# One region of fixed instruction order over the scans and output pipelines of a two-layer state-space kernel, with the pipelines' x chunks moved to the low end of SBUF

## The chip, the cores and the metric

The kernel runs on one core of a Trainium2 chip. The metric is device microseconds for one execution. The time before is the median of three runs. Profiles come from one further execution, with times counted from the start of its span.

## The reference, cut to what matters

Eight images of 64 x 64 pixels and 96 channels pass through two layers. Each layer normalizes over groups of channels, runs a selective scan in four directions over a map of 192 channels, normalizes over the channels, gates and projects back, and adds its input:

```python
x = x + _L0_conv_ref(_gn(x), ...)
x = x + _L1_conv_ref(_gn(x), ...)

# inside a layer, for the map xc (after projection, 3x3 convolution and silu):
dA = jnp.exp(d_t[..., None] * A)
h = dA * h + d_t[..., None] * B_e * u_t[..., None]     # over 4096 positions, 4 directions
y = sum(h * C_e)
y = _layernorm(y, norm_g, norm_b)
return y * _silu(z) @ out_proj_w.T
```

Layer 1 writes its scan with a cumulative sum, and only the first positions of each direction contribute beyond the skip term. The kernel computes those positions (4 x 160 of an image) as one "short" unit; everything else of layer 1 is its convolution, the skip term and the output.

## The kernel before, in words

**Stages.** After `begin` (the convolution and the first steps of image 0) a loop runs over the images. For image `b` it calls `scan_rows`, the scan of layer 0 for image `b` with the short unit of layer 1 for image `b - 1`, and then `between`, which calls `out_phase`: the output pipeline of layer 0 for image `b` and, from `b = 1` on, of layer 1 for image `b - 1`. `finish` takes the place of `between` for the last image. There are seven calls of `between`; the first has one stream, the other six have two.

**The scan.** Work comes in sets of 128 partitions (32 channels x 4 states) by 1024 positions, 384 sets for an image and 24 short ones (640 positions). For each set ACT makes `decay` (L801), DVE makes `set` by a product (L835; GpSimd does one set in four, L825) and scans it (L846; short sets L838 and L841), GpSimd multiplies by `c_rep` (L863), and PE sums over the states into `acc` (L887), which ACT copies to the map `y` (L918, short ones L907 to `y_short`). For each group of four sets ACT first copies `dtu_rep` to `drive` (L818). SP loads `dt_rep` and `dtu_rep` five sets ahead (L481) and `b_rep` and `c_rep` four ahead (L495), 512 KB each. At the end of the short unit, SP stores `y_short` to `ys_far` (L910): this is SP's last instruction of the scan.

**The pipeline.** `out_phase` cuts a map of 4096 positions into eight chunks of 512, so it has 16 chunks with two streams. Step `k` runs each stage for chunk `k` minus its lag: sum (GpSimd L1503, lag 0), mean (PE L1439, lag 1), centre (DVE L1516), square (ACT L1482), variance (PE L1460, lag 3), x load (SP L1568, lag 5), gates (PE L1453, lag 7), scale (DVE L1520, lag 8), affine (ACT L1487, lag 9), product (GpSimd L1512, lag 9), projection (PE L1472, lag 10), the last add (DVE L1611 for layer 0, L1557 for layer 1, lag 10) and the store (lag 11; SP L1613 for layer 0, ACT's queue L1558 for layer 1). A plan puts further stages at steps: the loads of the next image's map from `xc_far` (L1689, the first at step 0), its first projection (PE L514, step 2) and deltas (L556 to L619), the loads of `ys` and of `y1` (L1673, L1627), statistics of image `b + 2` (L1716), and the stages of the next group norms (L169, L179), the last of which, "root", stands at step 23 with a table load before it.

**What sets the order.** Inside `scan_rows` and inside `out_phase` a region `tc.manual_schedule()` makes each engine and queue issue its instructions in the order in which the program emits them. Each of these calls was a region of its own. Instructions outside them (the loads of `avg`, `pick` and `zw` at the head of `out_phase`, the memsets of `edged` at L1032), and where one region's instructions fall among those of the next on an engine, were left to the scheduler.

**Where things lie.** Pools are stacked from the low end of SBUF, those with `side="right"` from the high end. In the scan the low end holds, in this order, `rows` (`x_dbl0`), `beside` (`edged`, short tiles, `conv_out`), `piece` (states, `dt0`, `z0`, `ln0`, `dtu0`) and `work` (`set`, `out`); the loads are at the high end. In `between` the low end holds `behind` (`y1`, 32 KB of a partition) and then `final` (`pick`, `avg`, `zw`, x chunks in seven buffers of 2 KB, `sz`, `r`); the pool `before`, passed to `out_phase` as `brief`, is at the high end. A tile that takes the place of another waits until the last reader of that one is done.

The few lines that set the order:

```python
for k in range(max(n + 12, max(plan, default=0) + 1)):
...
    for stage, lag in order:
        if 0 <= k - lag < n:
            stage(k - lag)
...
    for stage in plan.pop(k, []):
        stage()
```

Of the kernel before, what the change touches and what calls it, by code (L numbers as in the profile page):

```python
# [8 lines left out]
F32 = mybir.dt.float32  # L9
# [6 lines left out]
NB, HH, WW, C = 8, 64, 64, 96  # L16
L = HH * WW
NH = 2
D = NH * C
# [3 lines left out]
MM = 512  # L23
# [24 lines left out]
def two_ss2d_layers(ctx: ExitStack, tc: tile.TileContext, t: dict, out: bass.AP):  # L48
# [13 lines left out]
    nc = tc.nc  # L62

    const = ctx.enter_context(tc.tile_pool(name="const", bufs=1))
    keep = ctx.enter_context(tc.tile_pool(name="keep", bufs=2))
# [72 lines left out]
    def load_late(pool, *names):  # L138
        for name in names:
            w[name] = pool.tile(list(t[name].shape), F32, name=f"w_{name}")  # L140
            nc.sync.dma_start(w[name], t[name])  # L141
# [1230 lines left out]
    def out_phase(*streams, plan=None, brief=None):  # L1372
# [9 lines left out]
        with (  # L1382
# [7 lines left out]
            chunks = L // MM  # L1390
            n = len(streams) * chunks
            brief = brief or pool
            load_late(pool, "avg", "pick")
            zw, zb = [], []
            for l, *_ in streams:
                zw.append(pool.tile([C, D], F32, name=f"zw{l}"))
                nc.sync.dma_start(zw[-1], t[f"in{l}"][:, D:])
                zb.append(pool.tile([C, NH], F32, name=f"zb{l}"))
            plan = plan(pmm) if plan else {}
# [155 lines left out]
    def finish_second(norm, y, chunk, dst):  # L1555
        def done(i, ps, x):
            nc.vector.tensor_tensor(x, ps, x, ALU.add)  # L1557
            return lambda: nc.scalar.dma_start(dst[:, i * MM : (i + 1) * MM], x)  # L1558

        return 1, norm, y, chunk, done  # L1560
# [1 line left out]
    def kept(x1T):  # L1562
        return lambda i, pool: x1T[:, i * MM : (i + 1) * MM]

    def loaded(src):
        def chunk(i, pool):
            x = pool.tile([C, MM], F32, name="x_in", bufs=7)
            nc.sync.dma_start(x, src[:, i * MM : (i + 1) * MM])  # L1568
            return x

        return chunk
# [32 lines left out]
                norm0[1] = first_norm(1, bank)  # L1604
        return xc, parts

    def finish_first(b, y, st):


        def done(i, ps, x):  # L1610
            nc.vector.tensor_tensor(x, ps, x, ALU.add)  # L1611
            chunk_stats(st, i, x)
            return lambda: nc.sync.dma_start(x1[b][:, i * MM : (i + 1) * MM], x)  # L1613

        return 0, norm0[b], y, loaded(t["x"][b]), done

    def short_sum(b, pool, brief, put):

        y1 = pool.tile([C, NH, L], F32, name="y1")
        ys = brief.tile([C, NH, HN], F32, name="ys")  # L1620
        rows = T // WW
        full, part = divmod(HEAD, HH)
        by_col = y1.rearrange("p h (a b) -> p h b a", b=WW)

        def load(i):
            at = slice(i * T, (i + 1) * T)
            nc.sync.dma_start(y1[:, :, at], xc1_far[b][:, :, at])  # L1627

        def scale(h, i):
            at = y1[:, h, i * T : (i + 1) * T]  # L1630
            nc.scalar.mul(at, at, w["dsum1"][:, h : h + 1])

        def patch(i):
            def add(dst, src):
                nc.vector.tensor_tensor(dst, src, dst, ALU.add)

            def segment(k, start, n):
                return ys[:, :, k * HEAD + start : k * HEAD + start + n]

            def columns(k, start):  # L1640
                cols = segment(k, start, full * HH).rearrange("p h (b a) -> p h b a", a=HH)
                return cols[:, :, :, at]

            at = slice(i * rows, (i + 1) * rows)
            if i == 0:
                add(y1[:, :, :HEAD], segment(0, 0, HEAD))
            if i == NT - 1:
                add(y1[:, :, L - HEAD :], segment(2, 0, HEAD))
            add(by_col[:, :, :full, at], columns(1, 0))
            add(by_col[:, :, WW - full :, at], columns(3, part))  # L1650
            if at.stop <= part:
                add(by_col[:, :, full, at], segment(1, full * HH + at.start, rows))
            if at.start >= HH - part:
                start = at.start - (HH - part)
                add(by_col[:, :, WW - full - 1, at], segment(3, start, rows))

        put(1, nc.sync.dma_start, ys, ys_far[b])
        for i in range(NT):
            put(1 + 2 * i, load, i)
            put(6 + 2 * i, scale, 0, i)  # L1660
            put(7 + 2 * i, scale, 1, i)
            put(7 + 2 * i, patch, i)
        return y1

    def second_of(b, pool, brief, put):

        return finish_second(norm1[b], short_sum(b, pool, brief, put), loaded(x1[b]), out[b])

    def planner():
        plan = {}  # L1670
# [6 lines left out]
    def between(b, y):  # L1677

        st = stats_tile()
        xc = keep.tile([C, NH, L], F32, name="map")  # L1680
        with (
            tc.tile_pool(name="before", bufs=1, side="right") as before,
            tc.tile_pool(name="behind", bufs=1) as pool,
        ):
            plan, put = planner()

            def load(i):
                at = slice(i * T, (i + 1) * T)
                nc.sync.dma_start(xc[:, :, at], xc_far[b + 1][:, :, at])  # L1689

            put(0, load, 0)
            streams = [finish_first(b, y, st)]
            if b >= 1:
                streams.append(second_of(b - 1, pool, before, put))
            for i in range(1, NT):
                put(7 + 2 * i, load, i)
            found = {}

            def beside(pmm):
                bank = lambda name: pmm.tile([P, MM], F32, tag="mm", name=name)  # L1700
                found["parts"], stages = first_deltas(b + 1, xc, before, pmm)
                steps = (2, 3, 3, 4) + (4, 5, 5, 6, 6, 7, 7, 6, 8, 9, 9)
                steps += (8, 9, 9, 10, 10, 11, 12, 14, 15, 16, 16) + (11, 12, 12, 13)
                for step, stage in zip(steps, stages, strict=True):
                    put(step, stage)
                stages, found[1] = group_norm_stages(st, bank)
                put(23, nc.scalar.preload_act_table_set, "natural_log_exp_and_others")
                for step, stage in zip((17, 18, 19, 20, 21, 23), stages, strict=True):
                    put(step, stage)
                if b + 2 < NB:  # L1710
                    ahead = stats_tile()
                    pieces = []

                    def piece(i):
                        pieces.append(before.tile([C, MM], F32, name="x_st", bufs=3))
                        nc.sync.dma_start(pieces[i], t["x"][b + 2][:, i * MM : (i + 1) * MM])  # L1716

                    for i in range(L // MM):
                        put(i + 3, piece, i)
                        put(i + 5, lambda i: chunk_stats(ahead, i, pieces[i]), i)  # L1720
                    stages, found[0] = group_norm_stages(ahead, bank)
                    for step, stage in zip((13, 14, 15, 16, 17, 18), stages, strict=True):
                        put(step, stage)
                return plan

            out_phase(*streams, plan=beside, brief=before)
            for kind, norm, image in ((1, norm1, b), (0, norm0, b + 2)):
                if kind in found:
                    norm[image] = tuple(found[kind][x] for x in ("gm", "r", "shift"))
        return xc, found["parts"]  # L1730

    def finish(b, y):

        st = stats_tile()
        with tc.tile_pool(name="behind", bufs=1) as pool:
            plan, put = planner()
            streams = [finish_first(b, y, st)]
            if b >= 1:
                streams.append(second_of(b - 1, pool, pool, put))
            out_phase(*streams, plan=lambda pmm: plan)  # L1740
        with tc.tile_pool(name="x1T", bufs=1) as pool1:
            x1T = pool1.tile([C, L], F32, name="x1T")
            nc.sync.dma_start(x1T, x1[b])
            xc = keep.tile([C, NH, L], F32, name="map")
            norm = conv_second(x1T, st, xc)
            with rotating():
                scan_head(xc, worst)
            out_phase(finish_second(norm, xc, kept(x1T), out[b]))
# [30 lines left out]
    x1 = dram.tile([NB, C, L], F32, name="x1")  # L1779
    xc_far, xc1_far, ys_far, xs, norm0, norm1 = ({} for _ in range(6))  # L1780
    xc, parts = begin()
    for b in range(NB):
        y = keep.tile([C, NH, L], F32, name="map")
        with (
            tc.tile_pool(name="rows", bufs=1) as rows,
            tc.tile_pool(name="beside", bufs=1) as pool,
        ):
            scan_rows(xc, y, parts, beside(b, pool), rows, pool)
        if b + 1 < NB:
            xc, parts = between(b, y)  # L1790
    finish(NB - 1, y)


# [98 lines left out]
```

## Time and profile before

| | us |
|---|---|
| median of 3 runs (12752.65 to 12780.65) | 12758.46 |
| the profiled execution | 12772.51 |
| its span | 12770.7 |
| DVE busy in it | 11379.4 (89%) |
| GpSimd busy | 10766.4 (84%) |
| ACT busy | 9763.0 (76%) |
| PE busy | 9506.4 (74%) |
| DMA queue of SP, share of 16 engines | 42.9% |

The boundaries between stages are read from the timeline: the last L863 (GpSimd) of a scan ends it, and the first L846 (DVE) begins the next. For the seven calls of `between`, in order:

| boundary | last L863 ends | first L846 starts | between them |
|---|---|---|---|
| 0 (one stream) | 1470.29 | 1567.63 | 97.3 |
| 1 | 2968.91 | 3126.45 | 157.5 |
| 2 | 4535.85 | 4690.75 | 154.9 |
| 3 | 6094.15 | 6247.41 | 153.3 |
| 4 | 7654.79 | 7806.21 | 151.4 |
| 5 | 9226.95 | 9380.58 | 153.6 |
| 6 | 10794.66 | 10948.80 | 154.1 |

In timeline lines an engine's name with a q (SPq, ACTq) is its queue, which issues DMAs; such a line shows the issue and not the transfer. A number in brackets at the end is the idle time of the engine before the instruction, with what ended it.

### The profile page before, as it was taken

To read this page: it belongs to the slowest core of one execution; us is meant where nothing else is said; L and a number is where in the kernel's file an instruction comes from. 1 tells how busy PE (TensorE), PEld (TensorE's weight loads), DVE (VectorE), ACT (ScalarE), POOL (GpSimd) and SP (SyncE) were. 2 spreads that over 40 slices of the span, in tenths; PEclk is the share of its full clock that TensorE was granted. 3 is DMA by queue.
4 is the path that set the end of the run, shared out by engine and by line. 5 is a ranking of instruction groups with operands and counts; after the bars stand their busy time and mean duration, and the time that the engine had idled before them with its cause. 6 is when DMAs were issued, how large, how long until landed. Compare 5 with 4: busy or idle time off the path is not lost. (4 is left out here: it accounts for less than half of the span.)

```text
span 12770.7 us, 135094 instructions
## 1 busy us (share of the span) xinstructions
PE 9506.4 (74%) x44284; PEld 2995.9 (23%) x44284; DVE 11379.4 (89%) x7387; ACT 9763.0 (76%) x14977; POOL 10766.4 (84%) x4884
## 2 busy tenths in 40 slices
PE   5875588876888678886787758888588885886556
PEld 1221122222222222222222212222122221222112
DVE  6999799997999979999799997999889998899976
ACT  4888788786787778877788867888678886788864
POOL 3999799986999869997799977999779996899964
PEclk8877688887887778877888878878688876887766
DMA  3444444443444444443444434444344443444430
GB/s 97 161 157 157 135 164 162 160 148 109 163 159 159 147 127 164 161 159 127 132 161 159 159 121 156 154 151 158 127 145 161 160 157 113 141 162 155 156 94 24
DMA packets 653799, 1839.45 MB, mean 144 GB/s; under 512 B 174408, under 2 KB 177870, under 8 KB 652989
## 3 DMA queue, kind: packets, MB, share of 16 engines
q1 hardware_dynamic: 645917, 1818.14, 42.9%
q10 hardware_dynamic: 7168, 12.59, 0.3%
q8 instruction: 351, 5.75, 0.2%
q14 instruction: 363, 2.97, 0.1%
HBM read 1524.94 MB, written 305.52 MB: 143 GB/s over the span
## 5 line engine op out<-in xcount | busy, mean ns | idle before, releaser
L863 POOL TENSOR_TENSOR out<-set,c_rep 128x1024 f32<-128x1024 f32 x3240 | 7472.8, 2325 | 1026.5 <-DVE set L846 342.1
L846 DVE TENSOR_TENSOR_SCAN set<-decay,state,set 128x1024 f32<-128x1024 f32 x2304 | 5365.2, 2345 | 415.1 <-ACT decay L801 182.0
L801 ACT ACTIVATE decay<-dt_rep,w_a 128x1024 f32<-128x1024 f32 x3240 | 3553.4, 1097 | 571.3 <-DVE set L846 330.7
L835 DVE TENSOR_TENSOR set<-drive,b_rep 128x1024 f32<-128x1024 f32 x2430 | 2864.3, 1179 | 27.5 <-DMA out<-x_in 16.3
L887 PE MATMUL acc<-out,w_gather 128*32 128x256 f32 x25920 | 2413.1, 485 | 548.2 <-ACT y_short L907 394.5
L955 PE MATMUL ps_conv<-edged,taps 96*96 96x512 f32 (+1 forms) x4032 | 2470.6, 752 | 42.9 <-ACT z L569 39.4
L825 POOL TENSOR_TENSOR set<-dtu_rep,b_rep 128x1024 f32<-128x1024 f32 (+1 forms) x810 | 1898.1, 2343 | 58.2 <-DMA dt_far<-ln 23.4
L846 DVE TENSOR_TENSOR_SCAN set<-decay,set 128x1024 f32<-128x1024 f32 x768 | 1743.3, 2285 | 148.1 <-ACT decay L801 78.5
L878 PE MATMUL acc<-map,w_eye 96*32 96x256 f32 x4608 | 567.1, 574 | 1480.5 <-ACT map L918 1244.1
L918 ACT COPY map<-acc 32x256 f32<-32x256 f32 x3072 | 1471.2, 479 | 49.9 <-PE acc L887 9.6
L887 PEld LDWEIGHTS acc<-out,w_gather 128*32 128x32 f32 x25920 | 843.6, 133 | 2539.2 <-issue 1459.8
L955 PEld LDWEIGHTS ps_conv<-edged,taps 96*96 96x96 f32 (+1 forms) x4032 | 724.8, 199 | 1390.9 <-issue 1218.7
L857 ACT COPY state<-set 128x1 f32<-128x1 f32 x2304 | 426.4, 185 | 776.8 <-DVE set L846 770.0
L588 PE MATMUL ps_sp<-z,w_eye 96*96 96x512 f32 x960 | 652.3, 767 | 286.9 <-ACT ln L597 243.3
L609 POOL TENSOR_TENSOR dtu<-ln,map 96x1024 f32<-96x1024 f32 x256 | 670.9, 2621 | 218.7 <-DVE ln L605 132.1
L818 ACT COPY drive<-dtu_rep 128x1024 f32<-128x1024 f32 (+1 forms) x810 | 796.9, 984 | 19.2 <-DVE set L835 10.9
L556 PE MATMUL ps_dt<-x_dbl,w_dtw 7*96 7x512 f32 x1024 | 593.7, 661 | 196.8 <-ACT z L569 150.4
L878 PEld LDWEIGHTS acc<-map,w_eye 96*32 96x32 f32 x4608 | 101.3, 121 | 1936.5 <-ACT map L918 1633.0
L588 PE MATMUL ps_sp<-dtu,w_eye 96*96 96x512 f32 x960 | 555.4, 663 | 0.0
L588 PE MATMUL ps_sp<-ln,w_eye 96*96 96x512 f32 x960 | 531.3, 637 | 0.0
L588 PE MATMUL ps_sp<-dt,w_eye 96*96 96x512 f32 x960 | 502.8, 606 | 0.0
L568 ACT ACTIVATE dt<-ps_dt 96x512 f32<-96x512 f32 x512 | 303.3, 592 | 250.5 <-PE ps_dt L556 231.8
(228 smaller groups left out, 9591.5 us busy)
## 6 DMA issues: line engine op xcount, KB each, us to landing
dt_rep<-dt_far SPq DMA_DIRECT2D x768, 512.0 KB
dtu_rep<-dtu_far SPq DMA_DIRECT2D x768, 512.0 KB
b_rep<-x_dblr SPq DMA_DIRECT2D x256, 512.0 KB
c_rep<-x_dblr SPq DMA_DIRECT2D x256, 512.0 KB
b_rep<-x_dblc SPq DMA_DIRECT2D x256, 512.0 KB
c_rep<-x_dblc SPq DMA_DIRECT2D x256, 512.0 KB
dt_far<-ln SPq DMA_DIRECT2D x256, 384.0 KB
dtu_far<-dtu SPq DMA_DIRECT2D x256, 384.0 KB
```

What stands on the lines that cost most here:

```text
L588: nc.tensor.matmul(job["ps"][:C, :], w["eye"], job[term][:, halves[s]], start=i == 0, stop=i == 3,)
L609: nc.gpsimd.tensor_tensor(like(job["dtu"], col), like(job["dt"], col), positions(xc[:, h, :], col, t0, T), ALU.mult,)
L801: nc.scalar.activation(s["decay"], s["group"]["dt"], AF.Exp, scale=rate)
L818: nc.scalar.copy(s["group"]["drive"], s["group"]["dtu"])
L825: nc.gpsimd.tensor_tensor(s["buf"], s["group"]["dtu"], b, ALU.mult)
L835: nc.vector.tensor_tensor(s["buf"], s["group"]["drive"], b, ALU.mult)
L846: nc.vector.tensor_tensor_scan(ordered(s["buf"], unit), ordered(s["decay"], unit), ordered(s["buf"], unit), 0.0 if unit["nth"] == 0 else s ...
L863: nc.gpsimd.tensor_tensor(s["out"], s["buf"], s["unit"]["c", s["i"]], ALU.mult)
L878: nc.tensor.matmul(acc, lhs[:, GC * g : GC * (g + 1)], positions(old[:, h, :], unit["column"], unit["t0"] + at, n), start=True, stop=False ...
L887: nc.tensor.matmul(acc, w["gather"], s["out"][:, at : at + n], start=s["i"] == 0 and unit["short"], stop=s["i"] == NS - 1, skip_group_chec ...
L918: nc.scalar.copy(yk, like(acc, unit["column"]))
L955: nc.tensor.matmul(job["ps"][:C, :], taps[l][:k, h, tap, :], edged[:k, tap // 3 : tap // 3 + rows, tap % 3 : tap % 3 + WW], start=tap == 0 ...
```

## The change

1. The whole loop over images, with the calls of `scan_rows` and `between`, stands inside one `tc.manual_schedule()`. The regions inside it remain. `begin` and `finish` stay outside.
2. The x chunks of `between` come from a new pool `xs`, opened before `behind`, so that it lies at the low end of SBUF and `behind` and `final` come after it. It has eight buffers instead of seven. In `finish` they come from `behind`.
3. `avg` and, with two streams, the `zw` of layer 0 move from `final` to `brief`.
4. The table load and root for layer 1's norm move from step 23 to step 24.

```diff
-            load_late(pool, "avg", "pick")
+            load_late(brief, "avg")
+            load_late(pool, "pick")
             zw, zb = [], []
             for l, *_ in streams:
-                zw.append(pool.tile([C, D], F32, name=f"zw{l}"))
+                home = brief if l == 0 and len(streams) > 1 else pool
+                zw.append(home.tile([C, D], F32, name=f"zw{l}"))
...
-    def loaded(src):
+    def loaded(src, xpool):
         def chunk(i, pool):
-            x = pool.tile([C, MM], F32, name="x_in", bufs=7)
+            x = xpool.tile([C, MM], F32, name="x_in", bufs=8)
             nc.sync.dma_start(x, src[:, i * MM : (i + 1) * MM])
             return x
...
             tc.tile_pool(name="before", bufs=1, side="right") as before,
+            tc.tile_pool(name="xs", bufs=1) as xpool,
             tc.tile_pool(name="behind", bufs=1) as pool,
...
-            streams = [finish_first(b, y, st)]
+            streams = [finish_first(b, y, st, xpool)]
             if b >= 1:
-                streams.append(second_of(b - 1, pool, before, put))
+                streams.append(second_of(b - 1, pool, before, xpool, put))
...
-                put(23, nc.scalar.preload_act_table_set, "natural_log_exp_and_others")
-                for step, stage in zip((17, 18, 19, 20, 21, 23), stages, strict=True):
+                put(24, nc.scalar.preload_act_table_set, "natural_log_exp_and_others")
+                for step, stage in zip((17, 18, 19, 20, 21, 24), stages, strict=True):
...
-    for b in range(NB):
-        y = keep.tile([C, NH, L], F32, name="map")
-        with (
-            tc.tile_pool(name="rows", bufs=1) as rows,
-            tc.tile_pool(name="beside", bufs=1) as pool,
-        ):
-            scan_rows(xc, y, parts, beside(b, pool), rows, pool)
-        if b + 1 < NB:
-            xc, parts = between(b, y)
+
+    with tc.manual_schedule():
+        for b in range(NB):
+            y = keep.tile([C, NH, L], F32, name="map")
+            with (
+                tc.tile_pool(name="rows", bufs=1) as rows,
+                tc.tile_pool(name="beside", bufs=1) as pool,
+            ):
+                scan_rows(xc, y, parts, beside(b, pool), rows, pool)
+            if b + 1 < NB:
+                xc, parts = between(b, y)
```

More of the change, by code (lines that the diff above doesn't have):

```diff
@@ L1605, in begin, with finish_first @@
         return xc, parts
-    def finish_first(b, y, st):
+    def finish_first(b, y, st, xpool):
         def done(i, ps, x):
@@ L1613, in done @@
             return lambda: nc.sync.dma_start(x1[b][:, i * MM : (i + 1) * MM], x)
-        return 0, norm0[b], y, loaded(t["x"][b]), done
+        return 0, norm0[b], y, loaded(t["x"][b], xpool), done
     def short_sum(b, pool, brief, put):
@@ L1663, in short_sum, with second_of @@
         return y1
-    def second_of(b, pool, brief, put):
-        return finish_second(norm1[b], short_sum(b, pool, brief, put), loaded(x1[b]), out[b])
+    def second_of(b, pool, brief, xpool, put):
+        return finish_second(norm1[b], short_sum(b, pool, brief, put), loaded(x1[b], xpool), out[b])
     def planner():
@@ L1736, in finish @@
             plan, put = planner()
-            streams = [finish_first(b, y, st)]
+            streams = [finish_first(b, y, st, pool)]
             if b >= 1:
-                streams.append(second_of(b - 1, pool, pool, put))
+                streams.append(second_of(b - 1, pool, pool, pool, put))
             out_phase(*streams, plan=lambda pmm: plan)
```

## The prediction

> **What bounds the kernel now.** I read the busy shares by stage first, since the page's averages mix stages. One period of the loop over images, here from the output pipeline of image 1 to the end of the scan of image 2 (columns: length, then busy time and count of PE, PEld, DVE, ACT, POOL, then clock and DMA):
>
> ```profile
> 2969.00:3127.00 158.00, 136.22 (x275) 41.61 (x276) 86.20 (x100) 109.55 (x162) 89.35 (x53) 0.85 0.51 149
> 3127.00:4438.00 1311.00, 1065.76 (x5070) 328.47 (x5068) 1235.40 (x711) 1054.50 (x1638) 1193.17 (x514) 0.81 0.46 154
> 4438.00:4536.00 98.00, 19.35 (x228) 9.44 (x232) 86.18 (x99) 52.30 (x81) 57.24 (x35) 0.50 0.20 67
> ```
>
> The scan (1311 us) is DVE's: 1235.4 us busy, 94%. The short sets (98 us) are DVE's too. Inside these two the order was already fixed before, and the change edits nothing there. The output pipeline (158 us) fills no engine's whole time: it is a chain from step to step, and what it costs beyond that lies at its two ends, where one region meets the next and where the scheduler could still choose. So I read both ends in the timeline, engine by engine.
>
> End of the pipeline, DVE, then ACT, then PE (columns: start, length, engine, line, operation, tiles, shapes, count, idle before and releaser):
>
> ```profile
> 3107.32 1.22 DVE L1520 TENSOR_TENSOR y<-y,ps_r 96x1024 f32<-96x1024 f32 x1 [0.17 <-PE ps_r L1444]
> ...
> 3121.14 0.69 DVE L1557 TENSOR_TENSOR x_in<-ps_out,x_in 96x512 f32<-96x512 f32 x1 [8.39 <-PE ps_out L1472]
> 3125.20 1.22 DVE L835 TENSOR_TENSOR set<-drive,b_rep 128x1024 f32<-128x1024 f32 x1 [3.37 <-DMA out<-x_in]
> 3126.45 2.29 DVE L846 TENSOR_TENSOR_SCAN set<-decay,set 128x1024 f32<-128x1024 f32 x1
> ```
> ```profile
> 3107.54 1.28 ACT L1673 ACT_TABLE_LOAD   x1 [0.70 <-DVE x_in L1557]
> ...
> 3108.94 1.00 ACT L818 COPY drive<-dtu_rep 128x1024 f32<-128x1024 f32 x1
> ...
> 3109.98 1.10 ACT L801 ACTIVATE decay<-dt_rep,w_a 128x1024 f32<-128x1024 f32 x1
> ...
> 3113.41 0.80 ACT L1487 ACTIVATE y<-y,w_lb,w_lg 96x512 f32<-96x512 f32 x1
> ...
> 3114.11 0.80 ACT L1487 ACTIVATE y<-y,w_lb,w_lg 96x512 f32<-96x512 f32 x1
> ...
> 3121.86 0.38 ACTq L1558 DMA_DIRECT2D out<-x_in  x1
> ```
> ```profile
> 3110.10 1.93 PE L1472 MATMUL ps_out<-y,w_out 96*96 96x512 f32 x4 [0.87 <-DVE x_in L1557]
> 3117.38 3.73 PE L1472 MATMUL ps_out<-y,w_out 96*96 96x512 f32 x4 [5.36 <-POOL y L1512]
> ```
>
> The reader is to see three things. The last chunk is scaled by 3108.54, but its affine starts only at 3113.41: a table load, the root of the next norm, one drive and two decays of the next scan stand before it on ACT. Its projection then runs on a PE that sat idle 5.36 us, in 3.73 us instead of 1.93. And DVE, free at 3121.83, waits until 3125.20 for the store of an x chunk to land, because the scan's `set` buffers lie on the memory of `x_in`.
>
> Start of the pipeline, SP (its first hoisted load belongs here too), then PE:
>
> ```profile
> 2789.87 0.59 SPq L1689 DMA_DIRECT2D map<-xc_far  x1
> ```
> ```profile
> 2969.83 0.33 SPq L141 DMA_DIRECT2D w_avg<-in_avg  x1
> 2970.21 0.42 SPq L141 DMA_DIRECT2D w_pick<-in_pick  x1
> 2971.02 0.31 SPq L910 DMA_DIRECT2D ys_far<-y_short  x1
> 2971.38 1.58 SPq L1397 DMA_DIRECT2D zw<-in_in  x2
> ```
> ```profile
> 2971.88 3.70 PE L1439 MATMUL ps_mean<-y_sum,w_avg 96*96 96x512 f32 x4 [2.16 <-DMA w_avg<-in_avg]
> 2975.37 2.85 PE L514 MATMUL ps_proj<-map,w_wx 96*78 96x512 f32 x4
> 2978.06 1.02 PE L1439 MATMUL ps_mean<-y_sum,w_avg 96*96 96x512 f32 x2
> ```
>
> Here the scheduler helps: the first map load goes out 180 us early, and `avg` passes ahead of the scan's last store, `ys_far`.
>
> [...]the affine ready at 3108.54 waited out what stood before it. [...]`avg` (36 KB) goes from issue to first use in 2971.88 - 2969.83 = 2.05 us[...]. [...]the trace shows 1.28 us and the next instruction 0.01 us later, so I use 1.28 alone.
>
> **The change part by part.** All of it by one boundary (image 1 to 2). The other five with two streams look alike: in all six the first L846 comes 151.4 to 157.6 us after the last L863, and the first L835 3.1 to 3.5 us after DVE's last add.
>
> *End, ACT order.* In emission order the affine of the last chunk comes before the table load and the root (now step 24, behind that step's affine) and before any drive or decay. So: affine at 3108.6, two of 0.80 overlapping, ends 3110.1; POOL's product, 2.35 us (its row in the timeline, 3114.99 to 3117.32), ends 3112.5; the projection follows the one before at 3112.02 by about 0.6 us, so PE is warm: 1.93, plus about 0.1 of passing on, 3114.6; DVE's last add 0.69, to 3115.3. Meanwhile ACT does the table load and root (1.28 + about 2.3 us for eight tiny ones, to 3113.7): hidden under product and projection; with no cover they would cost 3.6. Then ACT, in order, waits for the add to issue the last store (0.4, to 3115.7): behind this wait now stand drive and decays, and DVE waits for them. Drive 1.0, to 3116.7; L835 1.22; L846 starts at 3118.0 (decay, 1.1, is ready at 3117.8). Before: 3126.45. Gain **8.45 us**. Bounds: PE cold costs 1.8 back, a free pass 1.0 more: 5.5 to 9.5.
>
> *End, memory.* With `x_in` at the low end its buffers lie under `x_dbl0`, `edged`, the short tiles and the start of `piece`; `set` now lies on `y1`, read last by the projection. So the 3.37 us wait goes; drive is next late, as reckoned above, so it is inside the 8.45. The new neighbours: `x_dbl0` and `edged` sit on chunks 8 to 11, stored long before (their SP wait from 3109.69 to 3121.14 goes, off the path); the state and `dt0` may sit on chunks 14 and 15, whose store, issued at 3115.3, lands 3.1 later (3121.86 to 3125.0 before) at 3118.4, ahead of their first use at about 3118.8. Nothing; if late, 1 us.
>
> *Start, SP order.* After the scan's last instruction on SP, `ys_far` (waits for ACT until 3 us after L863's end, 2971.02), come `avg`, `pick`, `zw`, `zw`, then map load 0. `avg` is issued at 2971.4 behind 480 KB of `ys_far`; the `zw` issued there before landed at about 2974.2 to 2974.9 by the packets. So the first mean moves from 2971.88 to about 2974.2: **+2.3 us**. The map load goes out at about 2973.5; 768 KB at the 240 to 400 GB/s that the packets show are 2 to 3.2 us[...]: there at about 2978, when two means (3.5 us from 2974.2) are done. PE, in order, would hold the next means behind it. Bounds 0.5 to 4.7 (the upper: 6.3 us from issue to use, as the busier `dtu_rep` at 1558.54 to 1564.86, gives the third mean at 2982.7 instead of 2978.06). The pipeline is a chain, so I let all of it arrive at the end.
>
> *Together, at no cost:* `avg` and the first `zw` in the right-hand pool (their last readers, at steps 18 and 14, precede step 19's newton, after which SP's first `dt_rep` load, 3090.45, goes out); the eighth x buffer (SP's waits at L1568 shorten; gates waited 0.5 us in all for x, so nothing to win; loads of the scan, now behind the last x load, keep their 3090.45, and 12 loads of 512 KB at 400 GB/s are there by 3112, before 3116). With no cover the last x load held them 2.6 us at 3093.08, still in time.
>
> *Other boundaries.* Image 0 to 1 has one stream: its drive waits for a load (L818 at 1564.86), not for order or memory, and the mean waits for y_sum: zero, from -3 to +3. `finish` is outside the region: zero.
>
> *Sum:* 6 x (8.45 - 2.3) = **36.9 us**. The profiled execution took 12772.51 us (span 12770.7 and 1.8 around it): 12735.6. It lies 14.1 above the median of the runs, 12758.46; against that, 12721.5, so **12722**, -0.29%.
>
> **Rivals.** *Start is free*: if `avg` lands early and nothing queues, 6 x 8.45 = 50.7: 12708. For: first SP work in the right pool could be ready; against: program order behind `ys_far`.
> *Only the memory wait goes*: the affine stays late, drive then follows the store at 3121.83 + 0.4 + 1.05, L846 at 3124.5, gain 1.9, start 2.3: +0.4 x 6, 12761, no change. For: ACT has many waits in row; against: emission order leaves nothing ahead of the affine.
> *Slower: SP's queue holds PE.* All early loads stand in one queue behind `ys_far`, and PE's projection stands ahead of its means. If each of avg, map and y1 pays its full 5.7 us (map load: issued 2789.87, last packet 2795.56) in row, 3 x 5.7 - 2.3 already hidden = 14.8 per boundary, less 8.45: +6.3 x 6 = +38, 12796. It decides from 8.45 + 25.5 / 6 = 12.7 us on. For: strict SP order; against: the packets overlap, at 240 GB/s and more.
>
> **Chances.** Forecast 0.55, its own range 12707 to 12733 (net 4.2 to 8.5); free start 0.10; memory only 0.24; queue 0.11. The measurement tells 0.2% (25.5 us) from no change. Faster (under 12733): 0.63; within: 0.26 (memory only, and 0.02 of the forecast); slower: 0.11. Range 12700 (bounds 9.5 and 0.5, and some on image 0) to 12763.
>
> **What would show it.** Right: no wait of L835 on `out<-x_in`; affine of the last chunk within 0.2 us of its scale; its projection near 1.93; L846 some 9.5 us after that scale's end (17.9 before); map load 0 after `ys_far`, first mean some 5.3 us after L863's end (2.97 before). Wrong: a later affine, PE idle for the map load by more than 3 us, or a change inside the scan's 1311 us.

## The result, and the profile after

In runs of both kernels taken in turn, the changed kernel took 12780.78 us (median of 14, 12754.55 to 12836.28) and the kernel before 12769.17 (median of 14). The ratio is 1.0012, 95% interval 1.0000 to 1.0024: no gain, and if anything a small loss, where 0.29% less had been forecast. The profiled execution of the changed kernel took 12769.01 us, its span 12767.2.

In the code after, the lines of the pipeline stand 2 to 3 higher (L1487 is L1489, L1520 is L1522, L1689 is L1692); those of the scan are the same.

The stages of the same period first (columns as before: length, then busy time and count of PE, PEld, DVE, ACT, POOL, clock, DMA share, GB/s):

```profile
2974.80:3126.00 151.20, 126.69 (x272) 39.37 (x272) 85.76 (x100) 108.59 (x160) 88.38 (x51) 0.90 0.56 159
3126.00:4437.00 1311.00, 1061.31 (x5100) 329.24 (x5104) 1239.43 (x715) 1061.42 (x1648) 1194.93 (x517) 0.81 0.46 155
4437.00:4529.70 92.70, 15.89 (x200) 7.99 (x192) 82.42 (x95) 47.45 (x74) 55.41 (x33) 0.52 0.16 52
```

The scan is what it was: the seven scans that follow a boundary take 9837.5 us together, against 9839.4 before. The pipeline of this period is 6.4 us shorter. But the seven pipelines together are longer: 1031.8 us against 1022.2. So the answer lies in the pipelines, and differs from one to the next. (The two profiled spans differ the other way, by 3.5 us: all that lies outside the pipelines, most of it the first scan and what follows the last one, happened to take 13.1 us less in this one execution.)

The end of this pipeline, ACT, then DVE, then PE:

```profile
3116.12 1.52 ACT L1489 ACTIVATE y<-y,w_lb,w_lg 96x512 f32<-96x512 f32 x2 [1.74 <-DVE y L1522]
3117.52 0.32 ACTq L1560 DMA_DIRECT2D out<-x_in  x1
3117.88 1.28 ACT L1675 ACT_TABLE_LOAD   x1 [0.24 <-issue]
...
3123.12 0.32 ACTq L1560 DMA_DIRECT2D out<-x_in  x1
3123.48 1.02 ACT L818 COPY drive<-dtu_rep 128x1024 f32<-128x1024 f32 x1 [2.24 <-DVE x_in L1559]
```
```profile
3114.86 1.22 DVE L1522 TENSOR_TENSOR y<-y,ps_r 96x1024 f32<-96x1024 f32 x1 [0.17 <-PE ps_r L1446]
...
3122.40 0.69 DVE L1559 TENSOR_TENSOR x_in<-ps_out,x_in 96x512 f32<-96x512 f32 x1 [2.11 <-PE ps_out L1474]
3124.59 1.22 DVE L835 TENSOR_TENSOR set<-drive,b_rep 128x1024 f32<-128x1024 f32 x1 [1.50 <-ACT drive L818]
3125.92 2.29 DVE L846 TENSOR_TENSOR_SCAN set<-decay,set 128x1024 f32<-128x1024 f32 x1
```
```profile
3120.43 1.93 PE L1474 MATMUL ps_out<-y,w_out 96*96 96x512 f32 x4 [0.87 <-DVE x_in L1559]
```

The affine follows the last scale at once (3116.08 to 3116.12), the table load comes behind it, the projection takes 1.93 us (3.73 before), and `drive` waits for the last store: L846 starts 9.84 us after the last scale's end, 17.85 before (means of the six boundaries with two streams). The wait of L835 on the store of `x_in` is gone; `drive` is what it waits for now, 1.50 us.

The start of it, SP, then PE:

```profile
2976.89 0.31 SPq L910 DMA_DIRECT2D ys_far<-y_short  x1
2977.37 0.33 SPq L141 DMA_DIRECT2D w_avg<-in_avg  x1
...
2979.81 0.60 SPq L1692 DMA_DIRECT2D map<-xc_far  x1
```
```profile
2981.12 3.70 PE L1441 MATMUL ps_mean<-y_sum,w_avg 96*96 96x512 f32 x4 [5.54 <-DMA w_pick<-in_pick]
2986.75 3.67 PE L514 MATMUL ps_proj<-map,w_wx 96*78 96x512 f32 x4 [1.93 <-DMA map<-xc_far]
2990.21 1.21 PE L1441 MATMUL ps_mean<-y_sum,w_avg 96*96 96x512 f32 x2
```

The scan ends at 2974.8. `avg` is issued 2.6 us later, behind `ys_far`, and the map load 5.0 us later; it had gone out 180 us early before. PE's first mean comes at +6.3. (The bracket names `w_pick`, but this product reads `avg` alone, and `pick` is issued behind it on the same queue.) After the means PE stands for 1.93 us until the map load is there; over the six boundaries this stand is 1.9 to 2.7 us, and before there was none. The projection then takes 3.67 us (2.85 before), and the third mean starts at +15.4 instead of +9.2.

The granted clock, the share of its full speed that PE is allowed, tells the rest. The first 15 us of boundary 5, the worst of the six, and the 28.2 us after them, in the changed kernel, and then the same 28.2 us before:

```profile
9231.30:9246.30 15.00, 7.03 (x15) 2.02 (x16) 2.44 (x2) 3.29 (x6) 7.46 (x6) 0.50 0.76 194
9246.30:9274.50 28.20, 27.86 (x35) 6.52 (x34) 8.29 (x10) 10.85 (x16) 8.80 (x7) 0.50 0.61 158
```
```profile
9242.00:9270.20 28.20, 27.74 (x45) 6.91 (x44) 15.58 (x18) 23.47 (x31) 13.29 (x10) 0.70 0.66 175
```

PE is busy nearly all of the 28.2 us in both, but after the change at half clock throughout, with 35 matmuls done instead of 45. There PE is the bound: DVE, which waits for its means, was busy 8.29 us instead of 15.58. Over the kernel DVE's waits for the `ps_mean` of layer 0 grew from 157.4 to 217.2 us.

The six two-stream boundaries on average, in us after the end of the last L863:

| kernel | first mean | projection | third mean | fifth centre | last scale ends | L846 after that | sum |
|---|---|---|---|---|---|---|---|
| before | 2.97 | 6.46 | 9.27 | 17.87 | 136.30 | 17.85 | 154.15 |
| after | 6.18 | 12.21 | 15.67 | 26.88 | 146.05 | 9.84 | 155.89 |

The end gives 8.01 us and the start takes 9.75. From column to column these 9.75 are: 3.2 by the first mean (`avg` late), 2.5 more by the projection (PE's stand for the map load), 3.3 more by the fifth centre (PE at half clock), 0.7 after it. That is 6 x 1.74 = 10.4 us more; boundary 0 gives 0.9 back; 9.6 in all.

### The profile page after: what moved, and what is told of

Same layout as the page of the kernel before. It is cut to its first block, busy times and chain, and to the rows that moved or that the text cites. A ratio compares the mean times of both kernels' runs of the same rounds, so it can differ in the third digit from the quotient of the medians.

```text
span 12767.2 us, 135071 instructions
## 1 busy us (share of the span) xinstructions
PE 9506.2 (74%) x44284; PEld 2996.9 (23%) x44284; DVE 11381.4 (89%) x7387; ACT 9761.7 (76%) x14977; POOL 10760.4 (84%) x4884
## 3 DMA queue, kind: packets, MB, share of 16 engines
q1 hardware_dynamic: 645917, 1818.14, 43.2%
## 5 line engine op out<-in xcount | busy, mean ns | idle before, releaser
L863 POOL TENSOR_TENSOR out<-set,c_rep 128x1024 f32<-128x1024 f32 x3240 | 7467.8, 2323 | 977.9 <-DVE set L846 307.5
L846 DVE TENSOR_TENSOR_SCAN set<-decay,state,set 128x1024 f32<-128x1024 f32 x2304 | 5365.2, 2345 | 390.1 <-ACT decay L801 151.6
L835 DVE TENSOR_TENSOR set<-drive,b_rep 128x1024 f32<-128x1024 f32 x2430 | 2865.2, 1179 | 15.9 <-ACT drive L818 9.0
L846 DVE TENSOR_TENSOR_SCAN set<-decay,set 128x1024 f32<-128x1024 f32 x768 | 1744.3, 2286 | 167.7 <-ACT decay L801 87.8
L597 ACT COPY ln<-ps_sp 96x512 f32<-96x512 f32 x480 | 278.7, 581 | 279.0 <-PE ps_sp L588 272.0
```

The source lines that it names most:

```text
L835: nc.vector.tensor_tensor(s["buf"], s["group"]["drive"], b, ALU.mult)
L846: nc.vector.tensor_tensor_scan(ordered(s["buf"], unit), ordered(s["decay"], unit), ordered(s["buf"], unit), 0.0 if unit["nth"] == 0 else s ...
L863: nc.gpsimd.tensor_tensor(s["out"], s["buf"], s["unit"]["c", s["i"]], ALU.mult)
```

## The experiments

The theory after the result: the outer region pays at the start, because SP's queue keeps program order there and the map load lands in a crowd; the gain at the end comes from the other parts. The main rival: it is the clock or the memory layout, and not the queue. Each run was timed against the kernel before in the same sitting. There were four sittings, on two chips, so the ratios are to be compared and not the medians. The boundary columns come from one profiled execution of each run, as in the table above; that of e5 was the slowest of its 22 executions, that of e8 the fastest of its 12.

| kernel | first mean | projection | third mean | last scale ends | L846 after that | sum | median us | ratio to before, 95% |
|---|---|---|---|---|---|---|---|---|
| e1, after, store on ACT | 2.20 | 11.03 | 14.49 | 146.02 | 9.84 | 155.86 | 12763.67 | 1.0009 (1.0000 to 1.0019) |
| e2, after, map load early | 6.01 | 9.50 | 12.19 | 139.69 | 9.84 | 149.52 | 12733.65 | 0.9988 (0.9974 to 1.0002) |
| e3, both | 2.04 | 5.53 | 8.35 | 135.55 | 9.85 | 145.40 | 12705.66 | 0.9964 (0.9952 to 0.9976) |
| e4, after, no outer region | 2.03 | 5.52 | 8.22 | 135.18 | 8.24 | 143.43 | 12709.75 | 0.9964 (0.9951 to 0.9978) |
| e5, before, outer region | 6.15 | 12.33 | 15.80 | 152.62 | 14.75 | 167.37 | 12801.54 | 1.0024 (1.0014 to 1.0035) |
| e6, before, x at the low end | 2.95 | 6.45 | 8.97 | 137.07 | 15.55 | 152.62 | 12812.74 | 1.0035 (1.0022 to 1.0048) |
| e7, before, root at 24 | 2.96 | 6.45 | 9.23 | 135.89 | 12.02 | 147.91 | 12728.64 | 0.9970 (0.9961 to 0.9980) |
| e8, after, PE filled | 6.10 | 12.19 | 15.23 | 144.91 | 9.83 | 154.74 | 12782.41 | 1.0006 (0.9993 to 1.0018) |
| e9, e6 and avg, zw moved | 2.00 | 5.49 | 8.31 | 135.96 | 14.46 | 150.42 | 12753.06 | 0.9995 (0.9985 to 1.0006) |
| e10, e6 and root at 24 | 2.94 | 6.43 | 8.88 | 136.82 | 12.99 | 149.81 | 12800.35 | 1.0034 (1.0020 to 1.0049) |
| e11, after, PE filled longer | 6.10 | 15.09 | 16.81 | 144.14 | 9.84 | 153.98 | 12751.83 | 0.9988 (0.9975 to 1.0000) |

**e1: the last store of the scan on ACT's queue.**

```diff
-                nc.sync.dma_start(ys_far[unit["b"]], unit["y"])
+                nc.scalar.dma_start(ys_far[unit["b"]], unit["y"])
```

> The changed kernel with ys_far stored from ACT's queue, so that SP does not wait for it. Queue theory (the lost time is SP's queue at the start of the pipeline, behind ys_far): avg is issued about 1 us after the last L863 instead of 2.6, the first mean comes at about 3.5 to 4.5 us instead of 6.1 to 6.4, map load 0 at about 3 instead of 5.0, PE's first projection at about 9.5 instead of 12, the pipeline is 2 to 3 us shorter per boundary, in all 12 to 20 us. Rival, memory or clock of its own (the body of the pipeline is slower because of the new places in SBUF, or because the PE clock falls by chance): the first mean moves, the total of a boundary does not.

`avg` went out at once, the first mean came at 2.20, the map load was issued at +2.3. But the projection came only at 11.03, 1.2 us earlier than with the store on SP. In boundary 1 the load took 8.78 us from issue (3001.00) to use (3009.78), 6.94 in the changed kernel. These two stretches, the changed kernel first (the last three columns are clock, DMA share, GB/s):

```profile
2979.80:2986.70 6.90, 3.70 (x4) 0.96 (x4) 2.44 (x2) 1.65 (x2) 2.43 (x2) 0.50 0.94 238
```
```profile
3001.00:3009.78 8.78, 3.60 (x5) 0.86 (x5) 2.44 (x2) 2.11 (x2) 5.27 (x5) 0.50 0.97 261
```

In both the DMA engines are busy nearly all the time. So SP's wait for the store explains 1.2 us of the late projection and no more: issued 2.8 us earlier, the 768 KB load still has the store's 480 KB and the weights ahead of it or beside it. In time the run is the same as the changed kernel (1.0009 against 1.0012).

**e2 and e3: the first map load 365 sets into the scan; e3 with e1's edit too.**

```diff
+                def first_map():
+                    ahead[b + 1] = keep.tile([C, NH, L], F32, name="map")
+                    nc.sync.dma_start(ahead[b + 1][:, :, :T], xc_far[b + 1][:, :, :T])
+
+                plan.setdefault(365, []).append(first_map)
...
-        xc = keep.tile([C, NH, L], F32, name="map")
+        xc = ahead[b + 1]
...
-            put(0, load, 0)
```

> The changed kernel with map load 0 issued at step 365 of the scan, some 160 us before its end, as in the kernel before. Queue theory: avg and the first mean stay where they are (2.6 and 6.1 us after L863), PE's projection follows the second mean without waiting, at about 9.7 instead of 12, the third mean at about 12.5 instead of 15.5; 3 us per boundary, and more where PE's clock stays at half for less long; in all 18 to 40 us. Rival, memory or clock of its own: the third mean moves by 3 us, but the boundaries with a long half clock (2, 4, 5, 6) stay 4 to 11 us longer than in the kernel before.

> Both: ys_far from ACT's queue and map load 0 at step 365. Queue theory: start as before the change (mean at about 3 us, projection at 6.5, third mean at 9 to 10), end as in the changed kernel (L846 9.84 us after the last scale's end instead of 17.8), so six boundaries 8 us shorter than before: 12720 us, 0.38% faster than before, between 0.2 and 0.45%. The clock rises when it did before, since PE does not stand still. Rival, memory or clock of its own: the body stays 4 to 10 us longer in several boundaries, total within 0.2% of before.

With the load early, PE goes from the means to the projection with no wait in between, and the clock rises 9.8 to 12.7 us after the last L863 in all six boundaries (between 15.8 and 43.2 in the changed kernel, in three of them for 3.4 to 6.8 us only). From the projection to the fifth centre it takes 11.3 us, 14.7 in the changed kernel and 11.4 before. The late mean alone is carried on as it is: 3.4 us at the last scale (139.69 against 136.30). With both, the start is that of before and better; PE in boundary 1 of e3:

```profile
2986.01 3.70 PE L1447 MATMUL ps_mean<-y_sum,w_avg 96*96 96x512 f32 x4 [1.21 <-DMA w_avg<-in_avg]
2989.50 3.06 PE L514 MATMUL ps_proj<-map,w_wx 96*78 96x512 f32 x4
```

Here the scan ends at 2984.0: mean at +2.0, projection at +5.5. The kernel with the outer region is then 0.36% faster than before, and some 0.5% faster than the changed one (0.9964 / 1.0012). The two costs are not alike: the late map load alone (e1) costs the whole 9.7 us at the last scale, the late mean alone 3.4, and they overlap.

**e4: all of the change but the outer region.**

```diff
-    with tc.manual_schedule():
+    if True:
```

> The changed kernel without the outer region: x chunks low, avg and zw in the right pool, eight buffers, root at step 24, but the scheduler free between regions. Queue theory: map load 0 is hoisted again and the start is as before (mean 3.0, projection 6.5). End: the wait for the store of x is gone; if the scheduler again puts drive and decays ahead of the last affine, that costs up to 3.2 us, so L846 comes 10 to 14 us after the last scale instead of 17.8; 4 to 8 us per boundary, 24 to 48 us in all, 0.2 to 0.38% faster than before. Rival, memory: the pipeline's body is 4 to 10 us longer here too, and the total is that of before.

The scheduler sends the map load out 179 to 181 us early again, and `avg`, now in the right-hand pool, ahead of `ys_far`, at +0.03. The end is better too, 8.24 us instead of 9.84:

```profile
3127.80 0.69 DVE L1559 TENSOR_TENSOR x_in<-ps_out,x_in 96x512 f32<-96x512 f32 x1 [2.11 <-PE ps_out L1474]
3128.41 1.21 DVE L835 TENSOR_TENSOR set<-drive,b_rep 128x1024 f32<-128x1024 f32 x1
3129.72 2.29 DVE L846 TENSOR_TENSOR_SCAN set<-decay,set 128x1024 f32<-128x1024 f32 x1
```

L835 has no wait: ACT made `drive` 0.9 us ahead of the last scale's end and the decays between the tiny steps of the root, without waiting for the last store. So the outer region loses 12.5 us of a boundary, 155.89 - 143.43: 1.6 at the end, 10.9 at the start. And without the region the kernel is as fast as the best one with it (e3): 0.9964 both.

**e5 and e7: one part alone on the kernel before.** e5 has the outer region only, e7 the table load and root at step 24 only.

```diff
+    with tc.manual_schedule():
...
-                put(23, nc.scalar.preload_act_table_set, "natural_log_exp_and_others")
+                put(24, nc.scalar.preload_act_table_set, "natural_log_exp_and_others")
```

> The kernel before with nothing but the outer region. Queue theory: the start is that of the changed kernel (avg issued 2.6 us after the last L863, first mean 6.2, projection 12, third mean 15.5), so 6 us late and more where PE's clock stays at half. End: affine behind the table load and root of step 23 but ahead of drive and decays, ends some 4 us after the last scale; the store of x still has to land before L835, so L846 comes 14 us after that scale instead of 17.8. Per boundary 3 to 8 us more than before, in all 15 to 50 us slower, 0.1 to 0.4%. Rival, the region is harmless and memory costs: the time of the kernel before or less.

> The kernel before with only the table load and root at step 24. Start as before. The last affine follows its scale at once, as in the run without the outer region (ends 1.55 us after it), add ends at 7.0 instead of 13.3, but L835 waits for the store of x to land, 3.3 us later: L846 at 11.6 instead of 17.8: 6 us per boundary, 37 us, 0.29% faster. If the scheduler keeps drive and decays ahead of the affine, 3 us less per boundary.

e5 shows the same start as the changed kernel, though no tile was moved: so the late start comes from the order, and not from the new places in memory. Its clock is at half until 43 to 52 us in five of six boundaries, and it is slower than before by 0.24% (its profiled execution, 12841.83, lies 40 above its median, so its 167.37 is high). e7 is 0.30% faster: one number in a plan gives most of the gain at the end, 5.8 of 8.0 us. What is left in e7 is the wait for the store, which the new place of x takes away in e4; boundary 1 of e7:

```profile
3125.82 1.23 DVE L835 TENSOR_TENSOR set<-drive,b_rep 128x1024 f32<-128x1024 f32 x1 [3.60 <-DMA out<-x_in]
```

**e6, e9, e10: the place of x.** e6 has the pool `xs` and eight buffers only; e9 adds the move of `avg` and `zw`; e10 adds the root at step 24 to e6.

```diff
+            tc.tile_pool(name="xs", bufs=1) as xpool,
...
-            load_late(pool, "avg", "pick")
+            load_late(brief, "avg")
+            load_late(pool, "pick")
...
+                home = brief if l == 0 and len(streams) > 1 else pool
```

> The kernel before with only the x chunks in the pool at the low end, eight buffers; no outer region, avg and zw in final, root at step 23. Queue theory: start as before (mean 3.0, projection 6.5); L835 follows DVE's last add at once instead of 3.3 us later, L846 some 14.6 us after the last scale instead of 17.8: 3.3 us per boundary, 20 us, 0.16% faster. Rival, memory costs in the body: no gain or a loss.

e6 was the surprise: 0.35% slower, and not in the pipelines (10.5 us shorter in all) but in the scans, 9899.4 us against 9839.4. SP, then DVE, after boundary 2 of e6, and what SP waited for ahead of that first load (us in total, times, longest):

```profile
4701.53 0.56 SPq L481 DMA_DIRECT2D dt_rep<-dt_far  x1
...
4715.44 0.57 SPq L503 DMA_DIRECT2D x_dbl<-x_dblr  x1
```
```profile
4729.11 2.29 DVE L846 TENSOR_TENSOR_SCAN set<-decay,set 128x1024 f32<-128x1024 f32 x1 [11.56 <-ACT decay L801]
```
```profile
SPq L481 <- PE ps_r L1444: 22.4, 1, 22.4
```

The scan's first load goes out 8.9 us ahead of the first L846 (4710.38); before, it was 35 us. It waits for PE's L1444, which reads `pick` and `r` last; `r` lies above x and so, it seems, now in the place of `dt_rep`. The 12 loads of 512 KB all go out within the 14 us before `x_dbl` is asked for, PE's first deltas come 14.5 us after that L846 (3.5 in e9), and DVE loses 10 to 12 us in the second group of every scan; before, only in the one after the single-stream boundary. Nor is the wait of L835 gone here: it now waits 3.0 to 4.9 us for `b_rep`. Two readings: the place of `avg` and `zw`, which pushes what lies above x into the place of `dt_rep`, or the root at 23.

> The chunks of x in the low pool and avg and the first zw in the right-hand pool, the root still at step 23, no outer region. With only the chunks moved, SP's first dt_rep load went out 32 us after the last x load (some 9 us before the scan's first L846), its twelve loads were still landing when x_dbl was asked for, and DVE lost about 11.6 us in the group after, in every scan. Theory: avg and the first zw in the right-hand pool free the place that the dt_rep buffers wait for, so the loads go out some 26 us ahead of L846, the 11.6 us stall in the scan goes, and L846 comes 13 to 15 us after the last scale (the affine late, as before, but L835 no longer on a store or on b_rep): 12735 to 12755. Rival, that it is the root at step 23 that holds the loads: the stall stays in all scans, about 12810.

> The chunks of x in the low pool and the root at step 24, avg and the first zw where they were, no outer region. Theory that the place of avg and zw decides: dt_rep goes out late as with the chunks alone, L846 waits for b_rep some 13 to 15 us after the last scale though the affine is early, and the stall of about 11 us in the scan stays: 12790 to 12810. Rival, that the root at step 23 holds the loads: as with all parts but the outer region, about 12710.

e9 has the stall once in seven scans (10.8 us, after the single-stream boundary), e10 in all seven (9.2 to 11.5). In e10 SP waits for the same line as in e6; in e9 its first load goes out 31 to 32 us ahead of L846 in the six boundaries with two streams. So the small move of `avg` and `zw` is what makes the new place of x harmless: 1.0035 of before without it, 0.9995 with it. In e9 `drive` starts 0.40 us after the last scale, as with the affine late, and L846 at 14.46: the store's wait is gone and the rest of the lateness is ACT's order.

**e8 and e11: PE filled with products that nothing reads.**

```diff
+                    if n == 2 * chunks and brief is not pool and k in (0, 2):
+                        spare = po.tile([P, MM], F32, name="ps_out")[:C, :]
+                        for _ in range(3 if k == 0 else 1):
+                            nc.tensor.matmul(
+                                spare, w["eye"], part(7)[:, 0, :], start=True, stop=True
+                            )
```

> The changed kernel with four extra products of a 96x512 tile on PE at the start of each pipeline with two streams, three at step 0 (about 5 us at half clock, while PE waits for avg) and one at step 2 (while it waits for the map load); they go to a PSUM bank that nothing reads before step 10. If the long stretches at half clock in the changed kernel come from PE standing still in these waits, the clock rises in every boundary by about 12 to 16 us after L863 and stays up for more than 10 us, and the boundaries take 145 to 151 us like the better ones there: 20 to 40 us less than the changed kernel. If the clock follows something else, stretches of 10 to 27 us at half remain and the time stays within 10 us of it.

The clock rose early, at about 5 us in four of six boundaries, but fell to half again after 6.8 us in each of them, in two for 30.7 and 41.0 us, in two for 3.4. In these four the means at full clock were done sooner (four matmuls in 1.93 us in the fence below, 3.70 in the changed kernel), so PE stood all the longer for the map load, 2.86 to 3.40 us; boundary 1:

```profile
2980.35 1.93 PE L1441 MATMUL ps_mean<-y_sum,w_avg 96*96 96x512 f32 x4 [0.34 <-DMA w_pick<-in_pick]
2982.12 1.02 PE L1556 MATMUL ps_out<-map,w_eye 96*96 96x512 f32 x2
2986.44 3.67 PE L514 MATMUL ps_proj<-map,w_wx 96*78 96x512 f32 x4 [3.30 <-DMA map<-xc_far]
```

The wait had not been filled, and the run left the cause open. e11 has eight products in the second place instead of one.

> The changed kernel with eleven added 96x512 products on PE in each two-stream boundary, whose results nothing reads (added work): three where the first means wait for avg, eight between the means and the first projection. The run with one there left PE idle 3.30 us for the map load, and the clock, up by then, was half for some 30 us after. Theory that PE's stand ahead of the projection keeps the clock low: with it filled the clock, up at about 5 us after the last L863, stays up for 20 us and more in most of the six boundaries, the fourth centre comes at 21 to 23 us instead of 24 to 32, and the time is 12725 to 12755, though some products may push the projection 1 to 2 us out. Rival, that the fall of the clock doesn't hang on this stand: it falls after 7 us as before, the products at half clock (0.93 us each) push the projection out by up to 4 us, and the time is 12785 to 12810.

PE in boundary 1 of e11, and then the 30.8 us after the first 12 us of this boundary, in e8 and in e11:

```profile
2986.54 1.93 PE L1441 MATMUL ps_mean<-y_sum,w_avg 96*96 96x512 f32 x4 [0.33 <-DMA w_pick<-in_pick]
2988.30 7.03 PE L1556 MATMUL ps_out<-map,w_eye 96*96 96x512 f32 x16
2995.17 1.02 PE L514 MATMUL ps_proj<-map,w_wx 96*78 96x512 f32 x2
```
```profile
2986.20:3017.00 30.80, 30.22 (x37) 7.15 (x38) 8.08 (x10) 10.64 (x16) 10.14 (x9) 0.50 0.64 168
```
```profile
2992.40:3023.20 30.80, 29.52 (x56) 7.79 (x55) 9.91 (x12) 17.85 (x23) 11.39 (x10) 0.83 0.70 171
```

Now the clock rose at 5.2 to 5.9 us in five boundaries (10.5 in the sixth) and stayed up for 17 to 38 us in all six. From the projection to the fifth centre it took 10.3 us on average, 14.7 in the changed kernel and 11.4 before. The projection itself came 2.9 us later than in the changed kernel, since eight products were more than the gap, so the fifth centre came at 25.0 to 27.2 and not at the 21 to 23 expected (the centre called the fourth there is the fifth by count). Even so the kernel, with work added, comes out no slower and if anything faster than the changed one: 0.9988 against 1.0012 of before, with intervals that meet at 1.0000. The profiled boundaries show 6 x 1.91 = 11.5 us of it (0.09%); the rest isn't accounted for. What e8 and e11 show is the clock, not the time. PE's stand ahead of the projection is what delays its clock: with the stand gone, by an early load (e2) or by filling (e11), the clock comes up within 12.7 us of the last L863 in all six boundaries and stays up for 10 us and more. Half clock later in a pipeline has other causes too: e2 has stretches of 20.5 and 10.2 us of it, the kernel before of 17.1 and 10.2, with no such stand.

## Why the prediction was wrong

**End, ACT order and memory: right.** Put as times after the last scale's end, affine end 1.6 (measured 1.55), product 4.0 (3.97), projection 6.1 (6.28), last add 6.8 (7.01), `drive` 7.2 (7.40), L846 9.5 (9.84). Gain 8.01 instead of 8.45. The table load (1.28 us) and root were hidden, as assumed. Most of it needs no region: e7 gets 5.8 from the root's step alone.

**Start, SP order: the failed step.** It put +2.3 us, with an upper bound of 4.7; measured 6.4 at the third mean and 9.75 at the last scale. Three terms of it failed, worth 3.2, 2.5 and 3.3 us of the 9.75. The first mean was set at +2.3 and came +3.2 later. The map load was issued where I had it (4.6 after the scan's end, measured 5.0), but was to be there 4.5 us later, ahead of PE; it took 6.94, and PE stood for it. The wrong size is the transfer: I took the rates of packets elsewhere (2 to 3.2 us for the 768 KB), and the time until they start was an estimate of mine that no trace showed, while this load goes behind the store's 480 KB, `pick` and both `zw`, and with `ys` and `y1` on its heels, on engines that are 94% busy from its issue to its use. The 5.7 us that it took before, 180 us ahead of the seam, was already more than my 4.5, and I kept it for a rival only. And a third term was absent: what PE's stand does to its clock. I had read two projections, 1.93 and 3.73 us, at the end of the pipeline, and priced the slow one there (1.8 us), but not the same at the start, where PE is the engine that all wait for and the projection took 3.67 us. The sign that I set for this, PE idle for the map load by more than 3 us, did not appear (1.9 to 2.7): it priced the stand and not what the stand does to the clock.

**All of the start's cost arrives at the end: right**, and it is why the start decides: e2's 2.9 us at the third mean are 3.4 at the last scale, some 127 us later.

**Rivals.** "SP's queue holds PE" named the place and the chain. Its price of 14.8 us was too high, and the point of 12.7 from which it decides was not reached: 9.75 were enough to use up the gain, not to make the kernel 0.2% slower. "Start is free" is what happens without the outer region: e4 sends `avg` ahead of the store and saves 1.1 us at the last scale against before. "Only the memory wait goes" did not occur.

**At no cost: half right.** The eighth buffer and the loads behind the last x load show no cost in the changed kernel, though no run has them alone. The move of `avg` and `zw` costs nothing either, but I hadn't seen that it carries the new place of x (e6, e9, e10: 60 us of scan in e6). Boundary 0 moved by -0.9 us, inside the range given.

**Sums.** The prediction's 6 x (8.45 - 2.3) = 36.9 becomes 6 x (8.01 - 9.75) = -10.4. The parts nearly add up on the chip: in us per boundary, root alone -6.2, x with `avg` and `zw` alone -3.7, the three together -10.7, the outer region +12.5 on top of these and +13.2 on the kernel before (in a profiled execution that was long). Two figures of the prediction are off by themselves, and neither decides: `ys_far` waits for ACT until 2.1 us after the scan's end (2971.02 - 2968.91), not 3, and 8.45 less 1.8 for the slow projection is 6.65, not 5.5.

What stays open: why the clock, once held down, came back in boundary 1 after 15.8 us and in boundary 5 only after 43.2, with PE busy from the projection on in both. That the stand ahead of the projection delays it is shown (the changed kernel against e2, e8 against e11); by what rule it comes back is not. The length of the stand doesn't tell: in e1 PE stood for 5.0 to 5.2 us, twice as long, and the clock came back after 14.6 to 16.0 us in four boundaries and after 23.1 and 41.9 in two.

## What to carry to other kernels

A region of fixed order takes from the scheduler not only what it did badly but what it did well: list every DMA that it had hoisted (its issue lines lie far ahead of their stage), and place each by hand before closing the region; here that is the difference between 0.12% slower and 0.36% faster (e3). Ask too whether the region is needed at all: here the other parts without it gave the same 0.36% (e4). A load at a seam is priced by its landing in the crowd of that seam (here 6.94 us from issue to use, against 5.7 to the last packet when it went out 180 us early), and PE's stand there once more by its clock afterwards (14.7 us from the projection to the fifth centre with the stand, 11.3 without it in e2). Move a tile together with what lies above it: x moved alone cost 60 us of scan, in loads that the move didn't name.

## What the runs showed of the hardware

- PE's clock stayed at half for 28.2 us in which the profile counts PE busy for 27.86 (boundary 5 above). How long such stretches last, in us after the last L863: 3.4 (changed kernel, boundary 5, 53.5 to 56.9), 6.8 (changed kernel, boundary 6, 54.9 to 61.7), 10.2 (before, boundary 1, 32.3 to 42.5), 13.7 (changed kernel, boundary 6, 24.2 to 37.8) and 17.1 (before, boundary 5, 17.2 to 34.3). These are close to one to five times the shortest.
- In the four boundaries of e8 in which PE was at full clock when it came to its stand, the stand took 2.86 to 3.40 us and the clock fell in all four. How long it then stayed at half didn't follow the length: 30.7 us after a stand of 3.30, 41.0 after 3.40, but 3.4 after 3.34 and after 2.86. With the stand filled the clock stayed up (e11).
- A 768 KB load took 6.94 us from issue to use at the seam, and 8.78 when issued 2.8 us earlier there (e1), the DMA engines 94% and 97% busy: in that crowd 2.8 us of earlier issue bought 1.2.
